# Layer 0 of an attention network: v's projection rebuilt as three one-pass products of split operands, and moved behind the third query/key block

## The chip, the cores and the metric

The kernel runs on one core of a Trainium2 chip. A core has a matrix engine (PE; its weight loads are listed apart as PEld), a vector engine (DVE), an activation engine (ACT), a general engine (POOL) and a sync engine (SP), which issues most of the DMA transfers. The metric is the device time of one execution in microseconds, as a median over runs; less is better.

## The reference, cut to what matters

The network has two layers over eight images of 384 channels and 32 x 32 pixels (1024 tokens). The change touches layer 0 alone: group norm, one projection to q, k and v, attention with a bias that depends on relative position, an output projection and a residual.

```
tokens = gn(x).reshape(b, c, n).transpose(0, 2, 1)           # 8 x 1024 x 384
qkv = (tokens @ qkv_w + qkv_b).reshape(b, n, 3, 8, 48)       # q, k, v: 384 columns each
attn = softmax(q * 48**-0.5 @ k.T + relative_bias)           # per head, 1024 x 1024
x = x + (attn @ v).reshape(b, n, c) @ proj_w + proj_b
```

Layer 1 (another attention and a feed-forward part, both with layer norms) follows and is not changed.

## The kernel before, in words

**Layer 0, image by image.** For each image the loop at the end of `_layer0` runs 32 attention units: four pairs of heads, two halves of the queries, four key groups (`m2`, 256 keys). A unit is `scores` (line 692: PE products of k and q into two PSUM tiles; line 703: DVE adds the position bias from `grow` and writes the tiles `e`; line 707: ACT takes the exponential in place) and, two units later, `weigh` (line 723: PE multiplies `e` with v into a PSUM tile). `weigh` of unit i-2 stands between the score products of unit i and the exponentials of unit i, so it is queued on PE right behind them. Every fourth `weigh` ends a half: ACT copies one part of the sum to `oT` (line 731), DVE adds the other (line 734), and after two halves `divide` starts a chain of small transfers, a power on POOL (line 752), and two units later a product on POOL (line 768).

**The projections of the next image** are made between the last unit of one image and the first unit of the next; this stretch is called a transition here. There are seven. q and k of images 1 to 7 are computed exactly in three cheap products: an fp32 number is cut into a high part (mask the last 12 bits, line 108, DVE), a low part (subtract, line 630, DVE) and a mixed part (line 112, DVE)[...]. ACT copies the high part into an fp32r tile (line 625). q and k have 768 columns, that is six blocks of 128; `_Cut.products` (line 170) makes for a block and one part 6 matmuls (3 chunks of channels, 2 halves of 512 tokens), so 18 a block, into two PSUM tiles `pg` (high and low) and `pm` (mixed). ACT (line 646) and DVE (line 650) join them into the q and k tile. The weights were cut in the same way during image 0 (`_cut_weights`) and lie in DRAM; three of the six blocks fit into SBUF (tag "w"), and `cuts.load` fetches the others in turn.

**v** is different: `project_v` (line 666) multiplies the normalised image with the fp32 weights `wv` directly, 24 matmuls of 128 x 128 by 384 an image; each is two instructions in the trace (48 records). DVE adds the bias (line 671). Its four groups stand at three places of the transition: group 0 between the last score products and the two `weigh` calls still held, group 1 after these, groups 2 and 3 between the third and the fourth q/k block.

**What sets the order.** Each engine runs its instructions in the order written. `later` is a list of jobs, each due after a number of steps; `later.step()` is called once a unit, once a q/k block and once a v group. PSUM holds four tiles of 128 x 1024 (`shared.ps`), which scores, sums and projections share. The pool of `e` tiles has nine buffers; in a transition all nine parts of the image lie in it. The image itself lies in a tile with the tag "x", one buffer, in the shared pool.

Of the kernel before, what the change touches and what calls it, by code (L numbers as in the profile page):

```python
# [19 lines left out]
F32 = mybir.dt.float32  # L20
F32R = mybir.dt.float32r
AF = mybir.ActivationFunctionType
ALU = mybir.AluOpType
# [4 lines left out]
P = 128  # L28
QP = P // 2
B, C, IH, IW = 8, 384, 32, 32  # L30
N = IH * IW
KC = C // P
MT = N // P
HALF = 512
# [3 lines left out]
H0, D0 = 8, 48  # L38
S0 = 64
# [24 lines left out]
CUT = 4096.0  # L64
# [41 lines left out]
def _masked(nc, out, of):  # L106

    nc.vector.tensor_single_scalar(out.bitcast(INT), of.bitcast(INT), MASK, op=ALU.bitwise_and)


def _mixed(nc, out, low, high):
    nc.vector.scalar_tensor_tensor(out, low, -CUT, high, ALU.mult, ALU.add)
# [63 lines left out]
class _Shared:  # L176
# [13 lines left out]
    def mm2(self, name):  # L190
        return self.ps.tile([P, NH, HALF], F32, tag="p", name=name)
# [8 lines left out]
class _Weights:  # L200
# [74 lines left out]
def _layer0(tc, ins, x1, sums, shared, weights, beside):  # L275
# [9 lines left out]
    with ExitStack() as ctx:  # L285
# [8 lines left out]
        def etile(name, shape=(P, N), dtype=F32):  # L294
            return ep.tile(list(shape), dtype, tag="e", name=name)
# [298 lines left out]

        BB = len(BLOCKS) // 2
        cut = dram.tile([len(BLOCKS), P, 3, KC, P], F32, tag="cut", name="cut", bufs=1)

        def cut_tile(name):
            return etile(name)[:, 0 : 2 * C]

        class Ahead:

# [3 lines left out]
            def __init__(self, b, xn):  # L606
                self.b, self.xn = b, xn
                self.qk = {}

            def tile(self, pair):  # L610
                if pair not in self.qk:
# [6 lines left out]
            def mask(self, k):  # L618
                _masked(nc, self.high(k), self.xn[:, k])

            def highs(self):
                self.parts = [[], [], []]
                for k in range(KC):
                    t = etile(f"xh{self.b}_{k}", dtype=F32R)
                    nc.scalar.copy(t, self.high(k))
                    self.parts[0].append(t)

            def low(self, k):
                t = etile(f"xl{self.b}_{k}", dtype=F32R)
# [5 lines left out]
                _mixed(nc, t, self.parts[1][k].bitcast(F32), self.high(k))  # L635
                self.parts[2].append(t)

            def project(self, cuts, n, order):
                pair, s = BLOCKS[n]
                t = self.tile(pair)[:, s]  # L640
                name = f"{self.b}_{pair}_{s}"
                ps = mm2("pg" + name), mm2("pm" + name)
                for i in order:
                    cuts.products(n, i, ps[i // 2], self.parts[i])
# [14 lines left out]
                later.step()  # L659

        def project_v(b, xn, some=range(MT // 2)):
            for m2 in some:
                pv = mm2(f"pv{b}_{m2}")
                for i in range(2):
                    for k in range(KC):
                        nc.tensor.matmul(  # L666
                            pv[:, i, 0:C], xn[:, k, ts(2 * m2 + i, P)], wv[:, k, :],
                            start=(k == 0), stop=(k == KC - 1),
                        )
# [190 lines left out]
        for k in range(KC):  # L860
            stages = _cut_weights(
                nc, k, plain[:, ts(k, 2 * C)],
                lambda name, k=k: (
                    spare if name == "ch" else plain[:, ts(k, 2 * C)] if name == "cl"
                    else cut_tile(f"{name}0{k}")
                ),
                cut,
            )
            for at, stage in zip(((9, 11, 13, 15), (20, 21, 22, 23), (24, 25, 26, 27))[k], stages):
                later.after(at + 1, stage)  # L870
        for b in range(B):
            held = []
            for i, u in enumerate(units):
                done = held.pop(0) if len(held) == LAG else None
                held.append(
                    (u, scores(b, qk, u, lambda: weigh(b, *done) if done else None))
                )
                if i == (12 if b == 0 else 1) and b + 1 < B:
                    xn = load(b + 1)
                    for at, stage in zip(  # L880
                        (5, 6, 7, 10, 13, *((14, 15) if b == 0 else (13, 13))),
                        group_norm(b + 1, xn),
                    ):
                        later.after(at, stage)
                if i == 3 and b > 0:
                    project_out(b - 1, residuals(b - 1, etile), range(NF0))
                if b == B - 1:
                    for at, work in beside:
                        if at == i:
                            work()  # L890
                later.step()
                if i == 28 and b == 0:
                    cuts = _Cut(
                        nc, cut, BLOCKS,
                        shared.pool.tile([P, KC * 3 * C], F32R, tag="w", name="wc"),
                    )
                    for n in range(BB):
                        cuts.load(n)
                if b in (1, 2, 3) and i == 12:
                    t = cut_tile(f"cw{b}")  # L900
                    weights.load_part(b - 1, t)
                    for at, stage in enumerate(
                        weights.cut(
                            b - 1, t, lambda name, b=b, t=t: t if name == "cl" else cut_tile(f"{name}1{b}")
                        )
                    ):
                        later.after(4 + at, stage)
                if b + 1 < B and i in (28, 29, 31):
                    if i == 28:
                        ahead = Ahead(b + 1, xn)  # L910
                    ahead.mask((28, 29, 31).index(i))
# [12 lines left out]
            def project(some):  # L924
                for n in some:
                    ahead.project(cuts, n, (0, 1, 2) if n == order[0] else (2, 0, 1))
                    if n in order[:BB]:
                        cuts.load((n + BB) % len(BLOCKS))

            ahead.highs()  # L930
            for k in range(2):
                ahead.low(k)
            project_v(b + 1, xn, [0])
            weigh_held()
            ahead.low(2)
            weigh_held()
            ahead.mixed(0)
            project_v(b + 1, xn, [1])
            for k in range(1, KC):
                ahead.mixed(k)  # L940
            project(order[:BB])
            project_v(b + 1, xn, [2, 3])
            project(order[BB:])
            qk = ahead.qk

        for m in range(KC):
# [1350 lines left out]
```

## Time and profile before

| what | value |
| --- | --- |
| median of 3 runs | 2976.45 us (2976.02 to 2978.29) |
| the profiled execution | 2973.66 us, span 2971.8 us |
| mean granted PE clock | 0.998 |
| PE busy | 2940.6 us (99%), 19370 instructions |
| DVE, ACT, POOL busy | 1940.2 us (65%), 1507.2 us (51%), 489.8 us (16%) |
| v's projection in layer 0 (line 666) | 384 records, 8 images |
| cut products of both layers (line 170) | 1396 records |

The span is what the profile covers; the 1.9 us between it and the execution's own time lie around it. A busy PE is not PE at its peak, since its ends are modelled and matmuls overlap; the spacing of starts tells more. In a timeline a row is a run of like instructions: start, length from the first start to the last end, engine, line, operation, output and inputs, shapes, count, and in brackets the idle time before the row with what ended it.

### The profile page before, as it was taken

The numbers are of one execution on the slowest core, as the hardware profiler recorded it, in microseconds if no ns is written. First come the engines' busy times: TensorE is split into PE (matmuls) and PEld (weight loads), VectorE is DVE, ScalarE is ACT, GpSimd is POOL, SyncE is SP. The second block draws the span as 40 slices with busy tenths as digits, with TensorE's granted clock in tenths as the row PEclk, the third lists the DMA queues.
The fourth block names the chain that finished last, engine by engine and source line by source line (L and its number), as shares of the span: only waits on it lengthen the run. The fifth ranks groups of instructions, "written<-read, shape, count | busy, mean of one in ns | idle before, by whom it ended". The sixth has DMA issues, their size and how long they took to land.

```text
span 2971.8 us, 47061 instructions
## 1 busy us (share of the span) xinstructions
PE 2940.6 (99%) x19370; PEld 1662.5 (56%) x19370; DVE 1940.2 (65%) x1937; ACT 1507.2 (51%) x1846; POOL 489.8 (16%) x312
## 2 busy tenths in 40 slices
PE   8999999999999999999999999999999999999998
PEld 3345555656565655644545656746747747655553
DVE  3775748575675747564565785775775775875756
ACT  2654626354453626354463564564564555564644
POOL 3020202111110202112202202301302302302020
PEclk9999999999999999999999999999999999999999
DMA  7532131312203130222411112202202112112111
GB/s 196 171 99 85 44 111 38 97 59 52 76 16 112 24 104 24 63 89 60 128 50 38 61 38 67 85 17 79 73 25 77 68 31 71 67 40 82 40 45 38
DMA packets 129520, 203.71 MB, mean 69 GB/s; under 512 B 61872, under 2 KB 79648, under 8 KB 128816
## 3 DMA queue, kind: packets, MB, share of 16 engines
q1 hardware_dynamic: 126032, 198.77, 22.9%
q8 instruction: 156, 2.56, 0.4%
q10 hardware_dynamic: 3264, 1.82, 0.2%
q14 instruction: 68, 0.56, 0.1%
HBM read 152.99 MB, written 38.51 MB: 64 GB/s over the span
## 4 chain that ended last, share of the span: by engine, by line
PE 91%; DVE 3%; DMA 2%; ACT 2%; issue 1%; SPq 0%; POOL 0%; DVEq 0%; ACTq 0%
PE s L692 15%; PE o L723 14%; PE s L1649 11%; PE o L1698 10%; PE pg L170 6%; PE y2p L1943 6%; PE y1p L1892 5%; PE pp L791 4%; PE pv L666 4%; PE pv L1586 4%; PE pm L170 3%; PE pp L1795 3%; PE pq L1438 1%; PE pq L572 1%; DMA rb<-rd 1%
## 5 line engine op out<-in xcount | busy, mean ns | idle before, releaser
L707 ACT ACTIVATE e<-e 128x1024 f32<-128x1024 f32 x512 | 535.3, 1057 | 357.0 <-DVE e L703 339.9
L703 DVE TENSOR_TENSOR e<-s,grow 128x1024 f32<-128x1024 f32 x512 | 601.2, 1218 | 164.4 <-PE s L692 156.5
L692 PE MATMUL s<-qk 48*64 48x512 f32 x4096 | 615.0, 592 | 7.6 <-DVE e L703 7.5
L723 PE MATMUL o<-e,v 64*64 64x512 f32 x4096 | 609.1, 590 | 0.0
L1660 ACT ACTIVATE e<-s,kc 128x512 f32<-128x512 f32 x768 | 463.9, 694 | 173.0 <-PE s L1649 163.4
L1649 PE MATMUL s<-qk,qk 64*64 64x512 f32 x3072 | 418.9, 592 | 1.8 <-DVE oT L1708 1.6
L1698 PE MATMUL o<-e,v 64*64 64x512 f32 x3072 | 414.5, 590 | 0.0
L692 PEld LDWEIGHTS s<-qk 48*64 48x64 f32 x4096 | 228.9, 132 | 250.9 <-issue 104.3
L723 PEld LDWEIGHTS o<-e,v 64*64 64x64 f32 x4096 | 244.8, 133 | 196.9 <-issue 113.8
L1649 PEld LDWEIGHTS s<-qk,qk 64*64 64x64 f32 x3072 | 154.0, 132 | 191.9 <-issue 109.2
L1675 DVE TENSOR_TENSOR t<-t,e 128x1024 f32<-128x1024 f32 x192 | 230.9, 1221 | 45.8 <-ACT e L1660 45.8
L1698 PEld LDWEIGHTS o<-e,v 64*64 64x64 f32 x3072 | 159.9, 133 | 168.9 <-issue 141.8
L752 POOL TENSOR_TENSOR inv<-sums,over 128x16 f32<-128x16 f32 x32 | 95.6, 2988 | 866.3 <-DMA sums<-sd 591.4
L1879 DVE TENSOR_REDUCE parts<-y 128x1 f32<-128x1024 f32 x75 | 89.7, 1217 | 103.4 <-ACT y L1876 103.0
L1672 DVE TENSOR_TENSOR t<-e,e 128x1024 f32<-128x1024 f32 x96 | 114.1, 1224 | 59.5 <-ACT e L1660 59.5
L1555 POOL TENSOR_TENSOR hc<-hc,rsqrt 128x32 f32<-128x32 f32 x24 | 138.2, 5757 | 2.0
L666 PE MATMUL pv<-wv,xn 128*128 128x384 f32 x384 | 128.9, 490 | 0.0
L1586 PE MATMUL pv<-wv,bx 128*128 128x384 f32 x384 | 128.3, 491 | 0.0
L1795 PE MATMUL pp<-oT,L_attn_proj_wT 128*128 128x512 f32 x288 | 126.3, 595 | 1.5 <-DVE oT L1761 1.5
L791 PE MATMUL pp<-oT,wp 128*128 128x512 f32 x288 | 125.7, 595 | 0.0
L650 DVE SCALAR_TENSOR_TENSOR qk<-pg,qk 128x1024 f32<-128x1024 f32 x42 | 51.5, 1225 | 112.8 <-PE pg L170 98.1
L1586 PEld LDWEIGHTS pv<-wv,bx 128*128 128x128 f32 x384 | 119.4, 314 | 9.8 <-ACT e L1660 4.1
(213 smaller groups left out, 3507.7 us busy)
## 6 DMA issues: line engine op xcount, KB each, us to landing
rb<-rd SPq DMA_DIRECT2D x110, 256.0 KB
wc<-there SPq DMA_DIRECT2D x25, 576.0 KB
wc<-cut SPq DMA_DIRECT2D x24, 576.0 KB
xn<-in_x_dram SPq DMA_DIRECT2D x24, 512.0 KB
res<-in_x_dram SPq DMA_DIRECT2D x24, 512.0 KB
x<-res SPq DMA_DIRECT2D x24, 512.0 KB
bx<-x SPq DMA_DIRECT2D x8, 1536.0 KB
rq<-hi SPq DMA_DIRECT2D x48, 256.0 KB
```

The lines of the kernel that those rows point to most:

```text
L170: self.nc.tensor.matmul(out[:, h], w[:, i, k], part[k][:, ts(h, HALF)], start=(k == 0 and i != 1), stop=(k == KC - 1 and i != 0),)
L666: nc.tensor.matmul(pv[:, i, 0:C], xn[:, k, ts(2 * m2 + i, P)], wv[:, k, :], start=(k == 0), stop=(k == KC - 1),)
L692: nc.tensor.matmul(s[j][ts(c, QP), i], qk[pair][rows, 1, ts(4 * m2 + 2 * i + c, QP)], qk[pair][rows, 0, ts(h, HALF)], start=True, stop=True,)
L703: nc.vector.tensor_add(e.rearrange("p (i q) -> p i q", i=2), s[j], bass.AP(near.tensor, near.offset, [near.ap[0], [-QROWS * IW, 2], [1, HA ...
L707: nc.scalar.activation(e, e, AF.Exp)
L723: nc.tensor.matmul(po[ts(j, S0), r], v[keys, 2 * m2 + i, 2 * pair + j, :], es[j][keys, ts(i, HALF)], start=(m2 == 0 and i == 0), stop=(m2 ...
L791: nc.tensor.matmul(pps[b, m][:, h], (wp[:, k] if k < NF0 else wl)[:, ts(m, P)], oT[:, k, ts(h, HALF)], start=(k == 0), stop=(k == (NF0 if ...
L1586: nc.tensor.matmul(pv[:, i, 0:C], xt[:, k].rearrange("c (p m) -> c m p", m=MT)[:, 2 * m2 + i], wv[:, k], start=(k == 0), stop=(k == KC - 1),)
L1649: nc.tensor.matmul(s[j][ts(c, QP), i], qk[pair, 1][rows, ts(4 * m2 + 2 * i + c, QP)], qk[pair, 0][rows, ts(h, HALF)], start=True, stop=True,)
L1660: nc.scalar.activation(e[:, ts(i, HALF)], s[j][:, i], AF.Exp, scale=kc[:, pair, j, m : m + 1])
L1675: nc.vector.tensor_add(total[j], total[j], e)
L1698: nc.tensor.matmul(po[ts(j, D1), r], v[keys, 2 * m2 + i, at : at + D1], es[j][keys, ts(i, HALF)], start=(m2 == 0 and i == 0), stop=(m2 == ...
```

## The change

For images 1 to 7, v is now projected from the same three parts as q and k. In image 0, `cut_weights_v` splits `wv` chunk by chunk (DVE: mask, subtract, and two steps later mix and scale) and SP stores the parts in DRAM (`cut_v`). At the first transition the high part is loaded into the place of `wv` (tag "wv") and stays; the low and mixed parts are loaded at every transition into the tile with tag "x", that is over the image, once its low parts are made. `project_v` of `Ahead` makes 18 one-pass matmuls of 128 x 128 by 384 for each of four groups, into two PSUM tiles, and DVE joins them with two operations for each 128 tokens instead of one.

The order of a transition changes too. The two held `weigh` calls now follow the score products at once. Then come the high and low products of the first two blocks, their mixed products, the third block, all four groups of v, and the other three blocks. From image 1 on the masks move from units 28, 29 and 31 to 25, 26 and 27, and the fp32r copies of the high parts on ACT from the transition to units 28, 29 and 30; at the first transition they stay where they were.

```diff
+        def cut_weights_v(k):
+            w = wv[:, k]
+            t = etile(f"cv{k}")
+            high, mixed = t[:, 0:C], t[:, HALF : HALF + C]
+            def first():
+                _masked(nc, high, w)
+                nc.sync.dma_start(cut_v[:, 0, k], high)
+                nc.vector.tensor_sub(w, w, high)
+            def second():
+                _mixed(nc, mixed, w, high)
+                nc.sync.dma_start(cut_v[:, 2, k], mixed)
+                nc.vector.tensor_scalar_mul(w, w, CUT)
+                nc.sync.dma_start(cut_v[:, 1, k], w)
+            first()
+            later.after(2, second)
...
+            def load_weights_v(self, wh):
+                t = shared.pool.tile([P, KC, N], F32R, tag="x", name=f"wx{self.b}")
+                t = t.rearrange("p k n -> p (k n)")[:, 0 : 2 * KC * C]
+                nc.sync.dma_start(
+                    t.bitcast(F32), cut_v[:, 1:3].rearrange("p i k c -> p (i k c)")
+                )
...
+            def project_v(self, m2):
+                ps = [mm2(f"v{g}{self.b}_{m2}") for g in "gm"]
+                for i in range(2):
+                    for part in (2, 0, 1):
+                        for k in range(KC):
+                            nc.tensor.matmul(
+                                ps[part // 2][:, i, 0:C],
+                                self.parts[part][k][:, ts(2 * m2 + i, P)], self.wv[part][:, k],
+                                start=(k == 0 and part != 1), stop=(k == KC - 1 and part != 0),
+                            )
+                for i in range(2):
...
+                    nc.vector.scalar_tensor_tensor(
+                        to, pm, -1.0 / CUT, bv.rearrange("p (h d) -> p h d", d=D0),
+                        ALU.mult, ALU.add,
+                    )
+                    nc.vector.scalar_tensor_tensor(
+                        to, pg, 1.0 + 1.0 / CUT, to, ALU.mult, ALU.add
+                    )
+                later.step()
...
+        for k in range(KC):
+            later.after(17 + k, lambda k=k: cut_weights_v(k))
...
-                if b + 1 < B and i in (28, 29, 31):
+                masks, rounds = ((28, 29, 31), ()) if b == 0 else ((25, 26, 27), (28, 29, 30))
...
-            ahead.highs()
+            if b == 0:
+                wh = const.tile([P, KC, C], F32R, tag="wv", name="wvh")
+                nc.sync.dma_start(wh.bitcast(F32), cut_v[:, 0])
+                for k in range(KC):
+                    ahead.round(k)
             for k in range(2):
                 ahead.low(k)
-            project_v(b + 1, xn, [0])
             weigh_held()
             ahead.low(2)
+            ahead.load_weights_v(wh)
             weigh_held()
-            ahead.mixed(0)
-            project_v(b + 1, xn, [1])
-            for k in range(1, KC):
+            for k in range(KC):
                 ahead.mixed(k)
-            project(order[:BB])
-            project_v(b + 1, xn, [2, 3])
-            project(order[BB:])
...
+            for n in order[:2]:
+                for i in range(2):
+                    ahead.products(cuts, n, i)
+            for n in order[:2]:
+                ahead.products(cuts, n, 2)
+                ahead.take(n)
+                load_behind(n)
+            for at, n in enumerate(order[2:], 2):
+                for i in (2, 0, 1):
+                    ahead.products(cuts, n, i)
+                ahead.take(n)
+                load_behind(n)
+                if at == BB - 1:
+                    for m2 in range(MT // 2):
+                        ahead.project_v(m2)
```

More of the change, by code (lines that the diff above doesn't have):

```diff
@@ L596, in _layer0 @@
         cut = dram.tile([len(BLOCKS), P, 3, KC, P], F32, tag="cut", name="cut", bufs=1)
+        cut_v = dram.tile([P, 3, KC, C], F32, tag="cutv", name="cutv", bufs=1)
         def cut_tile(name):
             return etile(name)[:, 0 : 2 * C]
+        def cut_weights_v(k):
[13 more added lines that the diff above has]
+            later.after(2, second)
         class Ahead:
@@ L608, in __init__ @@
                 self.qk = {}
+                self.parts, self.ps = [[], [], []], {}
             def tile(self, pair):
@@ L619, in mask, with round @@
                 _masked(nc, self.high(k), self.xn[:, k])
[L621 to L626, printed above, removed]
+            def round(self, k):
+                t = etile(f"xh{self.b}_{k}", dtype=F32R)
+                nc.scalar.copy(t, self.high(k))
+                self.parts[0].append(t)
             def low(self, k):
@@ L636, in mixed, with products, take @@
                 self.parts[2].append(t)
-            def project(self, cuts, n, order):
+            def products(self, cuts, n, i):
+                if (n, i // 2) not in self.ps:
+                    pair, s = BLOCKS[n]
+                    self.ps[n, i // 2] = mm2(f"p{'gm'[i // 2]}{self.b}_{pair}_{s}")
+                cuts.products(n, i, self.ps[n, i // 2], self.parts[i])
+            def take(self, n):
                 pair, s = BLOCKS[n]
                 t = self.tile(pair)[:, s]
[L641 to L644, printed above, removed]
+                ps = self.ps.pop((n, 0)), self.ps.pop((n, 1))
                 by = D0**-0.5 if s == 0 else 1.0
@@ L659, in project, with project_v @@
                 later.step()
-        def project_v(b, xn, some=range(MT // 2)):
-            for m2 in some:
+            def load_weights_v(self, wh):
[4 more added lines that the diff above has]
+                )
+                t = t.rearrange("p (i k c) -> p i k c", i=2, k=KC)
+                self.wv = wh, t[:, 0], t[:, 1]
+            def project_v(self, m2):
[9 more added lines that the diff above has]
+                for i in range(2):
+                    to = v[:, 2 * m2 + i, :, SP:S0]
+                    pg, pm = (p[:, i, 0:C].rearrange("p (h d) -> p h d", d=D0) for p in ps)
+                    nc.vector.scalar_tensor_tensor(
[6 more added lines that the diff above has]
+                later.step()
+        def project_v(b, xn):
+            for m2 in range(MT // 2):
                 pv = mm2(f"pv{b}_{m2}")
@@ L907, in _layer0 @@
                         later.after(4 + at, stage)
-                if b + 1 < B and i in (28, 29, 31):
-                    if i == 28:
+                masks, rounds = ((28, 29, 31), ()) if b == 0 else ((25, 26, 27), (28, 29, 30))
+                if b + 1 < B:
+                    if i == masks[0]:
                         ahead = Ahead(b + 1, xn)
-                    ahead.mask((28, 29, 31).index(i))
+                    if i in masks:
+                        ahead.mask(masks.index(i))
+                    if i in rounds:
+                        ahead.round(rounds.index(i))
             def weigh_held():
@@ L922, in _layer0, with load_behind @@
             order = [n % len(BLOCKS) for n in range(b % 2 * BB, b % 2 * BB + len(BLOCKS))]
[L924 to L928, printed above, removed]
-            ahead.highs()
+            if b == 0:
[3 more added lines that the diff above has]
+                    ahead.round(k)
             for k in range(2):
                 ahead.low(k)
-            project_v(b + 1, xn, [0])
             weigh_held()
             ahead.low(2)
+            ahead.load_weights_v(wh)
             weigh_held()
-            ahead.mixed(0)
-            project_v(b + 1, xn, [1])
-            for k in range(1, KC):
+            for k in range(KC):
                 ahead.mixed(k)
-            project(order[:BB])
-            project_v(b + 1, xn, [2, 3])
-            project(order[BB:])
+            def load_behind(n):
+                if n in order[:BB]:
+                    cuts.load((n + BB) % len(BLOCKS))
+            for n in order[:2]:
[11 more added lines that the diff above has]
+                if at == BB - 1:
+                    for m2 in range(MT // 2):
+                        ahead.project_v(m2)
             qk = ahead.qk
```

## The prediction

> **What bounds the kernel now.** First the page's busy times:
>
> ```profile
> span 2971.8 us, 47061 instructions
> PE 2940.6 (99%) x19370; PEld 1662.5 (56%) x19370; DVE 1940.2 (65%) x1937; ACT 1507.2 (51%) x1846; POOL 489.8 (16%) x312
> ...
> PE 91%; DVE 3%; DMA 2%; ACT 2%; issue 1%; SPq 0%; POOL 0%; DVEq 0%; ACTq 0%
> ```
>
> PE is never idle for long, and the chain that ended last is 91% PE (last line). So PE work taken out of a transition comes off the end, if nothing then keeps PE waiting. Next the timeline of PE in the first transition (image 0 to 1), with ACT's rows in a second block:
>
> ```profile
> 188.81 0.59 PE L692 MATMUL s<-qk 48*64 48x512 f32 x1
> ...
> 190.97 2.16 PE L723 MATMUL o<-e,v 64*64 64x512 f32 x15
> 193.06 4.14 PE L666 MATMUL pv<-wv,xn 128*128 128x384 f32 x12
> 197.12 3.66 PE L723 MATMUL o<-e,v 64*64 64x512 f32 x32
> 200.72 4.14 PE L666 MATMUL pv<-wv,xn 128*128 128x384 f32 x12
> 204.40 1.84 PE L170 MATMUL pg<-xh,wc 128*128 128x512 f32 x6
> 206.08 1.56 PE L170 MATMUL pg<-xl,wc 128*128 128x512 f32 x6
> ...
> 217.28 7.90 PE L666 MATMUL pv<-wv,xn 128*128 128x384 f32 x24
> ...
> 237.70 5.92 PE L692 MATMUL s<-qk 48*64 48x512 f32 x45
> ```
>
> ```profile
> 192.77 2.20 ACT L707 ACTIVATE e<-e 128x1024 f32<-128x1024 f32 x2 [1.13 <-DVE e L703]
> 194.86 2.92 ACT L625 CAST xh<-qk 128x1024 fp32r<-128x1024 f32 x3
> ```
>
> Spacing: one record of v's fp32 matmul lasts 0.486 modelled, so 24 records are (7.90 - 0.486)/23 = 0.322 us apart. A one-pass product of 512 columns: (1.56 - 0.396)/5 = 0.233 us. From the first score product of unit 31 (188.81) to that of the next image (237.70) it is 48.89 us: scores and a `weigh` up to 192.97 (4.16), v 48 x 0.3225 = 15.48, two `weigh` 3.44, six blocks 108 x 0.2335 = 25.22, and some 0.6 at switches. The same interval in the other six transitions: 50.05, 48.84, 50.02, 49.91, 49.67, 49.55. What makes five of them longer is in the timeline of unit 30 of image 1:
>
> ```profile
> 355.51 2.37 POOL L768 TENSOR_TENSOR oT<-oT,rb 128x1024 f32<-128x1024 f32 x1 [6.37 <-DVE e L703]
> 356.53 1.91 DVE L108 TENSOR_SCALAR qk<-xn 128x1024 int32<-128x1024 int32 x1
> 359.62 1.51 PE L692 MATMUL s<-qk 48*64 48x512 f32 x11 [0.79 <-DVE e L703]
> ```
>
> The mask takes 0.68 elsewhere; here it ends 0.56 after POOL's product, so it stood behind it. The bias add behind the mask is late, and PE has no free PSUM tile. The same mask takes 1.88, 1.79, 1.56 and 1.43 in images 3 to 6. Last, DVE in image 0, units 17 to 20, where work is added:
>
> ```profile
> 141.79 2.36 DVE L703 TENSOR_TENSOR e<-s,grow 128x1024 f32<-128x1024 f32 x2 [0.39 <-PE s L692]
> 144.08 0.69 DVE L734 TENSOR_TENSOR oT<-o,oT 128x512 f32<-128x512 f32 x1
> 144.68 1.28 DVE L513 BATCH_NORM_STATS2 gst<-xn 128x6 f32<-128x512 f32 x2
> 145.88 2.34 DVE L703 TENSOR_TENSOR e<-s,grow 128x1024 f32<-128x1024 f32 x2
> 148.13 1.27 DVE L513 BATCH_NORM_STATS2 gst<-xn 128x6 f32<-128x512 f32 x2
> 149.33 2.34 DVE L703 TENSOR_TENSOR e<-s,grow 128x1024 f32<-128x1024 f32 x2
> 152.57 1.23 DVE L703 TENSOR_TENSOR e<-s,grow 128x1024 f32<-128x1024 f32 x1 [0.90 <-PE s L692]
> ```
>
> Here DVE runs without a gap from 141.79 to 151.67; it, not PE, sets the pace.
>
> [...] In the trace the first two loads of a v group are 0.108 us apart[...]
>
> **The change part by part.**
>
> *v's products.* Out: 15.48 us a transition. In: 4 groups x 18 = 72 one-pass matmuls of 384 columns, a form the trace doesn't have. [...] Upper end: the 233.5 of 512 columns, if it isn't the columns that set it. I take 178: 12.82 us, so 2.66 less, times 7: **-18.6**. Ends: [...]233.5 gives +9.3.
>
> *The masks.* At units 25 to 27 no POOL product runs in the transitions shown (it comes in unit 30); POOL's power in unit 27 (3 us) didn't hold a DVE scaling of 0.55 that ran inside it in image 0 (179.97). The five long transitions lose their excess over 48.87: 1.18 + 1.15 + 1.04 + 0.80 + 0.68 = **-4.8**. Ends: -4.8 and 0 (mask 25 falls behind an `oT` sum and another POOL operation holds it).
>
> *The copies of the high parts.* Three a transition go to units 28 to 30 on ACT, 0.95 us apart in a row. A unit lasts 3.44 us and ACT needs 2 x 1.06, at most 0.59 for `oT`, and now 1.0: 3.7 once, 3.2 otherwise. The exponentials of unit 31 begin when DVE has added (ACT idles 1.1 us before them now), so they aren't later. Zero; end +1 a transition (7) if they are.
>
> *No v group ahead of the held `weigh` calls.* Behind the last copy of the exponentials now stands `weigh` of unit 31: PE ends unit 29's at 192.97 and unit 30's at 194.69, but ACT ends the last exponential at 192.77 + 2.20 = 194.97. PE waits some 0.35. DVE's low parts (from 194.32, 1.15 apart, third after unit 30's `weigh`) are done about 198; PE needs them 1.4 us after `weigh` 31's end at 196.8. Mixed parts follow DVE's `oT` sum, from about 198.5 to 202; PE has 4 x 1.4 = 5.6 us of high and low products of two blocks before them, up to 202.4. In transition 1, where the copies still follow the exponentials, the third ends at 197.8, needed at 197.8. The third block takes over the PSUM tile of the first one's mixed product; from the start of those 6 products ACT begins 1.74 later (207.48 to 209.22) and takes 1.12, against 2.80 for both mixed products: 0.15. Switches between types drop from 0.6 to 0.3. Net 0.2 x 7: **+1.4**; ends 0 and +7.
>
> *The weights of v.* 1.18 MB issued on SP when the third low part is made, about 9 us into the transition, behind no other wait; needed after two `weigh`, three blocks: 4.16 + 3.44 + 54 x 0.2335 + 0.5 = 20.7. Three loads of 590 KB moved from 183.9 to about 192 with some other traffic, 250 to 300 GB/s, so 4 to 5 us and 2 of latency: there at 16. If it were late, it would cost its lateness seven times. SP's `sd` and q/k stores queue behind it, and these wait for DVE results that come later anyway. The block loads are issued earlier than before, and have v's 12.8 us to land in. The first transition adds 590 KB ahead of it, under the same cover.
>
> *Joining v.* 4 DVE operations a group, near 0.55 each (128x384 addition: 0.553), 2.2 us under 3.2 us of PE; before, 1.1 of 3.9. Hidden.
>
> *Cutting wv in image 0.* Per chunk on DVE: mask and scale (0.55 at 768 columns, 0.68 at 1024, so 0.35 at 384), subtract and mix (0.95 and 1.22, so 0.545): 1.8 us, 1.45 at back-to-back spacing. They come after the bias additions of units 16 (first of chunk 0), 17, 18 (also the second of chunk 0), 19 and 20. Unit 16's, 0.8, has a gap of 0.39 ahead; those of 17 and 18, 0.8 and 1.6, none; unit 19's falls into the gap of 0.90, unit 20's mostly into one of 0.6. Exposed: 0.4 + 0.8 + 1.6 + 0.2 = **+3.0**; ends +1.5 and +5.5 (all of it). The nine stores (1.77 MB, units 17 to 21) hold three `e` buffers, about two units each; the next users come three units later.
>
> Sum: -18.6 - 4.8 + 1.4 + 3.0 = -19.0. On the profiled execution 2973.66 (span 2971.8 and 1.9 around it) that gives 2954.7. The median lies 2.8 above that execution, and I carry the offset: 2976.45 - 19.0 = **2957.4**.
>
> **Rivals.** *A product of 384 columns costs what one of 512 does.* 72 x 0.2335 = 16.8 us, 1.3 more than v now: +9.3 instead of -18.6, total +8.9, 2985. [...] Against: a load is only 0.108 us[...]. It decides from a spacing of (15.48 + 0.06)/72 = 0.216 us on, where the whole gain is gone. *v's weights late*: at 100 GB/s, as the mixed traffic about 225 moved, 12 us and 2 of latency put them at 23, 2.3 late x 7 = 16: 2973. Against: the large contiguous loads ran at 250. *ACT and DVE can't hold the end of the attention*: no gain from masks (4.8) and 1 us lost a transition (7): 2969. *The cheaper product isn't reached by the path*, since DVE and ACT become the bound in the transition: they were busy 18.7 and 10.1 of the 45 us from 195 to 240, and DVE gets 8 operations of 0.55 more. Discarded.
>
> **How the numbers follow.** Main case 0.79: 2951 to 2964 by its bounds. Rival 1 0.07, rival 2 0.05, rival 3 0.06, the rest 0.03, both ways. Range 2949 to 2969. This measurement can't tell less than 0.2%, 6 us, from nothing. Faster: the main case, rival 3 and a part of rival 2, 0.87; same 0.05; slower 0.08.
>
> **What would show it.** The new v rows: 36 matmuls of 384 columns, spacing 0.176 to 0.180 us. Transitions near 46.4 us, alike to 0.3. No mask over 0.7 in units 25 to 27 and no PE wait for DVE in unit 30. A wait of 0.2 to 0.5 before the last `weigh`. In image 0 three longer units, 17 to 19. Wrong if the spacing is over 0.2, if PE waits for a DMA before v's first product, or if score products wait for DVE in units 26 to 30.

## The result, and the profile after

The changed kernel takes 2957.8 us (median of 6 runs, 2955.07 to 2959.49) against 2977.37 for the kernel before beside it (6 runs, 2974.22 to 2979.95): 0.9934 of its time, with a 95% interval of 0.9923 to 0.9946. The forecast was 2957.4. Beside each other the two medians differ by 19.6 us, where 19.0 was forecast. Repeated on another chip, further down, the ratio was 0.9934 again (0.9920 to 0.9947).

The total agrees to 0.4 us, but the transitions and image 0 are each off by about 3 us, with opposite signs. The spans of the two profiled executions differ by 18.8 us, and three stretches account for it:

| stretch | before | after | difference | forecast |
| --- | --- | --- | --- | --- |
| seven transitions, first score product of unit 31 to that of the next image | 346.9 us | 321.8 us | -25.1 us | -22.0 us |
| image 0, first score product of unit 0 to that of unit 31 | 113.4 | 119.3 | +5.9 | +3.0 |
| start of image 0 | 75.4 | 75.9 | +0.5 | 0 |

The page of the changed kernel, the same lines as were shown of before:

```profile
span 2953.0 us, 47525 instructions
...
PE 2920.5 (99%) x19538; PEld 1694.0 (57%) x19538; DVE 1970.4 (67%) x2005; ACT 1505.0 (51%) x1846; POOL 491.5 (17%) x312
...
PE 91%; DVE 3%; DMA 2%; ACT 2%; issue 1%; SPq 0%; POOL 0%; DVEq 0%; ACTq 0%
```

The chain is still 91% PE and PE is still busy 99% of the time: 20 us of its work are gone, and no other engine has taken over. The timeline of PE in the first transition (start, length, engine and line, operation, shapes, count):

```profile
197.31 5.98 PE L777 MATMUL o<-e,v 64*64 64x512 f32 x47
...
216.17 0.69 PE L698 MATMUL vm<-wx,xd 128*128 128x384 f32 x3
...
228.66 1.55 PE L170 MATMUL pm<-xd,wc 128*128 128x512 f32 x6
```

All 72 products of v, one record each where an fp32 product of v had two, stand in one block, from 216.17 to 228.66: 12.49 us, so 0.1735 us each (0.1733 in the next transition), against 15.48 us for v before. No row of this stretch, up to the next image's first score product at 241.34, has an idle time in brackets. The row from 197.31 holds the last three `weigh` calls, the two held ones among them. Its products start in groups of four, 0.43 us from group to group. One distance differs: the first group of the last `weigh` starts 0.77 us after the group before it (200.58 to 201.35). That is the wait for the last exponential, 0.34 us, and it is 0.34 in each of the seven transitions; the row shows no gap for it because the records before it, with their modelled ends, reach over it. ACT's row of that exponential, which ends at 201.30:

```profile
199.11 2.19 ACT L761 ACTIVATE e<-e 128x1024 f32<-128x1024 f32 x2 [1.13 <-DVE e L757]
```

The timeline of DVE at the end of image 1's attention, with the masks in their new units (the last one is shown):

```profile
352.54 0.68 DVE L108 TENSOR_SCALAR qk<-xn 128x1024 int32<-128x1024 int32 x1
...
360.58 2.35 DVE L757 TENSOR_TENSOR e<-s,grow 128x1024 f32<-128x1024 f32 x2 [0.33 <-PE s L746]
```

This is the mask of unit 27; those of units 25 and 26 take 0.68 and 0.69 us, where one had taken 1.91. POOL's product of unit 30 (359.32 to 361.70) meets none of them, and DVE then waits for PE, not PE for DVE. Last, DVE in image 0, within units 19 to 22:

```profile
152.04 0.54 DVE L112 SCALAR_TENSOR_TENSOR cv<-wv,cv 128x384 f32<-128x384 f32 x1
152.62 0.36 DVE L616 TENSOR_SCALAR wv<-wv 128x384 f32<-128x384 f32 x1
...
155.16 0.55 DVE L112 SCALAR_TENSOR_TENSOR cv<-wv,cv 128x384 f32<-128x384 f32 x1
...
163.57 1.23 DVE L757 TENSOR_TENSOR e<-s,grow 128x1024 f32<-128x1024 f32 x1 [2.18 <-PE s L746]
```

The first two lines, chunk 0, are what the forecast described: mixing (line 112) and scaling (616) stand between other work on a DVE that had no gap, and the bias additions come later. The third is the mixing of chunk 1. The pieces take 0.35 to 0.56 us, as estimated. The last line isn't in the forecast: one bias addition comes after DVE has stood idle for 2.18 us. The trace names the score product as what it waited for, but that had ended at 159.80, so another semaphore was the last. The addition writes an `e` buffer. The queue of SyncE shows who held it (line 818 loads for the division, line 615 stores parts of v's weights):

```profile
157.48 1.09 SPq L818 DMA_DIRECT2D rb<-rd  x2
158.66 0.53 SPq L615 DMA_DIRECT2D cutv<-cv  x1
```

The second store of chunk 1 (line 615) reads that buffer. Its data, the third line above, were ready on DVE at 155.71, but it was issued at 158.66, behind the division's store (155.73) and loads (157.48). PE's unit 22 lasts 6.18 us instead of 3.57. The lengths of image 0's units 16 to 23, from the starts of their score products:

| kernel | 16 | 17 | 18 | 19 | 20 | 21 | 22 | 23 |
| --- | --- | --- | --- | --- | --- | --- | --- | --- |
| before | 10.38 | 3.61 | 3.66 | 3.75 | 3.45 | 3.44 | 3.57 | 4.16 |
| after | 10.56 | 3.67 | 3.97 | 4.60 | 5.18 | 3.69 | 6.18 | 4.06 |

Units 17 to 21 are 3.2 us longer, most of it in units 18 to 20, and unit 22 is 2.6 us longer.

### The profile page after: what moved, and what is told of

It reads as the page before. It is cut to its first block, busy times and chain, and to the rows that moved or that the text cites. A ratio compares the mean times of both kernels' runs of the same rounds, so it can differ in the third digit from the quotient of the medians.

```text
span 2953.0 us, 47525 instructions
## 1 busy us (share of the span) xinstructions
PE 2920.5 (99%) x19538; PEld 1694.0 (57%) x19538; DVE 1970.4 (67%) x2005; ACT 1505.0 (51%) x1846; POOL 491.5 (17%) x312
## 4 chain that ended last, share of the span: by engine, by line
PE 91%; DVE 3%; DMA 2%; ACT 2%; issue 1%; SPq 0%; POOL 0%; DVEq 0%; ACTq 0%
PE s L746 15%; PE o L777 15%; PE s L1722 11%; PE o L1771 11%; PE pg L170 6%; PE y2p L2016 6%; PE y1p L1965 5%; PE pp L845 4%; PE pv L1659 4%; PE pm L170 3%; PE pp L1868 3%; PE vg L698 2%; PE pq L1511 2%; PE pq L572 1%; PE vm L698 1%; DVE qk L1592 1%
## 5 line engine op out<-in xcount | busy, mean ns | idle before, releaser
L1745 DVE TENSOR_TENSOR t<-e,e 128x1024 f32<-128x1024 f32 x96 | 114.1, 1224 | 57.7 <-ACT e L1733 57.7
L1965 PE MATMUL y1p<-lun,w 128*128 128x512 f32 x360 | 113.5, 396 | 2.4 <-DVE lun L1915 2.4
```

Of the source, the lines that this page charges most:

```text
L1965: nc.tensor.matmul(py[m][:, h], w1[:, k, ts(m, P)], un[k][i][:, ts(h, HALF)], start=(k == 0 and i == 0), stop=(k == KC - 1 and i == 1),)
```

## The experiments

Times are medians, ratios are to the kernel before on the same chip with the 95% interval. The transitions of each kernel that bears on them, in us:

| kernel | 0-1 | 1-2 | 2-3 | 3-4 | 4-5 | 5-6 | 6-7 | sum |
| --- | --- | --- | --- | --- | --- | --- | --- | --- |
| before | 48.89 | 50.05 | 48.84 | 50.02 | 49.91 | 49.67 | 49.55 | 346.9 |
| masks early alone | 48.88 | 48.82 | 48.82 | 48.82 | 48.80 | 48.81 | 48.81 | 341.8 |
| changed, v in fp32 | 49.15 | 48.91 | 48.97 | 48.91 | 48.93 | 48.89 | 48.93 | 342.7 |
| changed | 46.19 | 45.92 | 45.97 | 45.93 | 45.96 | 45.89 | 45.94 | 321.8 |
| changed, masks late | 45.72 | 46.96 | 47.19 | 46.99 | 47.54 | 47.18 | 46.84 | 328.4 |
| changed, not interleaved | 47.78 | 47.03 | 47.01 | 47.01 | 46.99 | 47.00 | 47.01 | 329.8 |
| changed, v's weights late | 52.75 | 51.57 | 52.62 | 51.71 | 52.87 | 51.84 | 53.07 | 366.4 |

**Masks early, alone**

```diff
-                if b + 1 < B and i in (28, 29, 31):
-                    if i == 28:
+                masks = (28, 29, 31) if b == 0 else (25, 26, 27)
+                if b + 1 < B and i in masks:
+                    if i == masks[0]:
```

> The kernel before with one edit: in images 1 to 6 the three masks of the next image's x stand behind units 25, 26, 27 instead of 28, 29, 31. Nothing else of the change is in it. The prediction's step 2: the stretches from unit 31 to the next image of 50.05, 50.02, 49.91, 49.67 and 49.55 us fall to 48.8 to 48.9, because no mask overlaps GpSimd's multiply any more (each mask 0.68 to 0.70 us), the two of 48.84 stay, units 25 to 27 stay at 3.44: 4.8 us less in all, 2972 to 2973. Rival A, the end of attention has no room (R3): units 25 to 27 grow by 0.2 to 0.7 each in six images, 4 to 10 us given back, 2974 to 2982. Rival B, the long stretches come from something else (transfers, the take): they stay between 49.5 and 50.1, 2977.

Measured: 2968.74 us, 0.9978 (0.9968 to 0.9988), 6.0 us below the kernel before beside it (2974.78). The transitions of images 1 to 6 are all 48.80 to 48.82, and units 25 to 27 stay at 3.44. That is 5.2 us less in the transitions, where 4.8 was forecast; both rivals fall. The span of this execution is 6.0 us shorter too; of the rest, 0.3 is in the start of image 0 and 0.6 behind layer 0's last image, where the edit changes nothing.

**Masks and copies late**

```diff
-                masks, rounds = ((28, 29, 31), ()) if b == 0 else ((25, 26, 27), (28, 29, 30))
+                masks, rounds = (28, 29, 31), ()
...
-                for k in range(KC):
-                    ahead.round(k)
+            for k in range(KC):
+                ahead.round(k)
```

> The changed kernel with its steps 2 and 3 undone: masks behind units 28, 29, 31 and the three fp32r copies on ScalarE behind unit 31, in all images; the cut of v's weights, its products and their order stay. By the prediction's step 2 the stretches of 45.9 to 46.2 us of images 1, 3, 4, 5, 6 grow by 0.7 to 1.2 each and that of image 2 by nothing: 4.8 us more than the changed kernel, near 2962.5; a mask near a GpSimd multiply takes 1.2 to 1.8 us instead of 0.68. Rival A, the copies' move was worth something too: the six stretches all grow, by 0.5 to 1 each beyond that, 2965 to 2969. Rival B, what the changed kernel gained was v's products alone, and the order of masks is hidden: within 1 us of the changed kernel, 2957 to 2959.

Measured: 2963.14 us, 0.9955 (0.9939 to 0.9970). Against the changed kernel the six transitions that the edit touches grew by 1.04, 1.22, 1.06, 1.58, 1.29 and 0.90, which is 7.1. (The first one, which it leaves as it was, came out 0.5 shorter; why is not shown.) Rival B falls. Rival A expected the copies to cost on top of the masks. The lengths of the masks show that they don't. This is the timeline around unit 30 of image 1 in this kernel:

```profile
362.78 2.38 POOL L822 TENSOR_TENSOR oT<-oT,rb 128x1024 f32<-128x1024 f32 x1 [6.37 <-DMA rb<-rd]
...
364.00 1.70 DVE L108 TENSOR_SCALAR qk<-xn 128x1024 int32<-128x1024 int32 x1
```

The mask takes 1.70 us, 1.01 over its 0.69. In the six images the masks of unit 29 exceed 0.69 by 1.01, 1.16, 1.04, 1.56, 1.26 and 0.85 us; each transition's growth is within 0.06 us of its mask's. So the masks explain all of it but 0.06 us a transition at most, and the move of the copies is worth no more than that; zero was forecast. What I had wrong in the expectation is image 2: here its mask collides too (1.85 us). In the kernel before, that mask started at 526.69 and POOL's product at 526.70; the mask took its 0.68, and it was the product that took longer, 2.91 us instead of 2.38. In this kernel the product starts first, at 529.99, and the mask at 531.08. In both kernels the one that started second took longer than it does elsewhere. This kernel's profiled execution is the longest of its four, 2969.16 us, and its image 0 took 122.2 us, which the note on the clock below comes back to.

**v in fp32 at its new place**

```diff
-                    for m2 in range(MT // 2):
-                        ahead.project_v(m2)
+                    project_v(b + 1, xn)
```

The cut of v's weights in image 0 and the loads of its parts are not in this kernel either, since nothing uses them.

> The changed kernel with v's projection as one fp32 product again (48 matmuls of 128x384), at its new place behind the third block; v's weights are not cut in image 0 and not loaded. Masks, copies and the interleaved first two blocks stay as in the changed kernel. The forecast's account: the v part of a transition takes 15.4 to 15.5 us instead of 12.48, so each of the seven stretches is 3.0 us longer, 48.9 to 49.0; image 0 goes back from 119.3 to 113.4 between unit 0 and unit 31. Against the changed kernel 21.0 - 5.9 = 15 us more, 2973, and 4 to 5 below before. Rival A, the order and not the parts brought the gain (interleaving, v behind the third block): 2958 to 2965. Rival B, the longer units of image 0 have nothing to do with the cut: image 0 stays near 119, 2978 to 2979.

Measured: 2970.01 us, 0.9981 (0.9973 to 0.9990), 4.8 us below the kernel before beside it. The transitions sum to 342.7, 20.9 above the changed kernel: 2.99 each. Image 0 takes 113.4 us again. From v's first product to the second row behind v's block it is 395.22 - 378.36 = 16.86 us here, and 396.08 - 382.22 = 13.86 in the changed kernel:

```profile
378.36 15.64 PE L720 MATMUL pv<-wv,xn 128*128 128x384 f32 x48
...
395.22 1.10 PE L170 MATMUL pg<-xh,wc 128*128 128x512 f32 x4
```

The gain is the product of v itself, and both rivals fall. Set beside the kernel with early masks alone, this one is 0.9 us worse in its transitions: the new order with the old product isn't a gain.

**The first two blocks not interleaved**

```diff
-            for n in order[:2]:
-                for i in range(2):
-                    ahead.products(cuts, n, i)
-            for n in order[:2]:
-                ahead.products(cuts, n, 2)
-                ahead.take(n)
-                load_behind(n)
-            for at, n in enumerate(order[2:], 2):
-                for i in (2, 0, 1):
+            for at, n in enumerate(order):
+                for i in (0, 1, 2) if at == 0 else (2, 0, 1):
```

> The changed kernel with the first two blocks' products not interleaved by parts: each block runs high, low, mixed (the later ones mixed, high, low) before the next begins. The mixed parts of x are ready at 10.5, 11.7 and 12.9 us after unit 31's first score and the first block asks for them at 10.8: TensorE waits 0.4 to 0.6 us twice, 1.0 to 1.2 us in each of seven transitions, and they take 47.0 to 47.2 us instead of 45.9; 7 to 8 us more than the changed kernel, 2965 to 2966. Rival, the wait is met by slack elsewhere (the take of the first block begins earlier and frees its sums earlier): within 1 us of the changed kernel, 2957 to 2959.

Measured: 2964.81 us, 0.9956 (0.9939 to 0.9973); transitions +8.0 in all. The timeline of PE in the second transition shows where:

```profile
374.36 0.73 PE L170 MATMUL pm<-xd,wc 128*128 128x512 f32 x2 [0.24 <-DVE xd L112]
375.50 2.13 PE L170 MATMUL pm<-xd,wc 128*128 128x512 f32 x8 [0.40 <-DVE xd L112]
```

PE asks for the second and the third chunk of the mixed parts before DVE has made them. The starts of consecutive products are 0.63 and 0.80 us apart there instead of 0.23: 0.97 us, of the 1.11 that the transition grew. In the kernel before, a group of v stood between the two held `weigh` calls and the first block, so PE had other work at this place. I read the interleaving as paying for the wait that moving v opens; no run tests it without that move.

**v's columns divided otherwise**

```diff
+                    for at, end in (((0, C),), ((0, 192), (192, C)), ((0, 256), (256, C)), ((0, 320), (320, C)))[m2]:
...
-                                ps[part // 2][:, i, 0:C],
+                                    ps[part // 2][:, i, at:end],
```

> The changed kernel with the columns of v's one-pass products divided otherwise in each of the four groups of a transition: first group 384 as it is; second 192 and 192; third 256 and 128; fourth 320 and 64. The distance of products tells what a column costs. If a product costs in proportion to its columns (233.5 ns at 512, 173.3 at 384, so 0.45 to 0.46 ns each): 320 take 144 to 147 ns, 256 take 115 to 117, and below some 108 ns, where the load of 128x128 weights takes longer than the product, 192, 128 and 64 columns all cost about 108. The groups then take 18 x 173 = 3.1 us, 36 x 108 = 3.9, 18 x (116 + 108) = 4.0 and 18 x (146 + 108) = 4.6. Rival A, a fixed part in each product (173.3 and 233.5 give 0.47 ns per column, so a fixed part of minus 7: this would need another form): 256 and 320 columns lie off the line by over 10 ns. Rival B, no floor from the weight load: 192 cost 87 ns, 128 cost 58, 64 cost 29, and all groups take 3.1 us.

This kernel was run for the distances alone (one execution, 2980.06 us). The timeline of PE in the second transition, rows of two sizes, each with the row behind it:

```profile
386.81 0.68 PE L699 MATMUL vm<-wx,xd 128*128 128x384 f32 x3
387.33 0.68 PE L699 MATMUL vg<-wvh,xh 128*128 128x384 f32 x3
...
397.40 0.60 PE L699 MATMUL vg<-wx,xl 128*128 128x320 f32 x3
397.84 0.42 PE L699 MATMUL vm<-wx,xd 128*128 128x64 f32 x3
```

A row is three products, so the distance of two starts by three is what one costs: 0.173 us for 384 columns, 0.147 for 320, and by rows read in the same way 0.117 for 256. From 384 columns down to 256, and with the 0.2335 of 512 last, that is 0.451, 0.458, 0.457 and 0.456 ns a column: in proportion, without a fixed part. Below that a floor holds. Products of 192 columns came 0.111 to 0.113 us apart, and those of 64 and 128 columns 0.111 to 0.112 where they follow their own kind. The four groups took 3.13, 4.00, 4.10 and 4.62 us, as the main account of the expectation had it, and both rivals fall. That the load of the weights sets the floor fits the 0.108 us between the first two loads of a v group in the kernel before, but no run tests it alone.

**v's weights loaded late**

```diff
             ahead.low(2)
-            ahead.load_weights_v(wh)
...
                 ahead.take(n)
+                if n == order[0]:
+                    ahead.load_weights_v(wh)
```

> The changed kernel with the load of v's low and mixed weights (1.18 MB) issued behind the first block's take instead of ahead of the last weigh. The stores of that take are issued some 18 us after unit 31's first score, so the load is issued at about 19 and lands 5.1 us later, at 24, while the products ask for it at 20.8. Account: TensorE waits 3 to 4.5 us ahead of v's products in each of seven transitions, which take 49 to 50.4 us instead of 45.9: 21 to 31 us more, 2979 to 2989. This is the prediction's rival R2 made to happen. Rival, the load is not what v's products wait for (the wait shown by the trace is for sums or VectorE): transitions within 1 us of 45.9, 2957 to 2965.

Measured: one execution, with a span of 3001.6 us against 2953.0, outside both expectations. The wait itself is as expected: in the trace's list of what waited for the tile `wx`, v's products stand 28.6 us in seven waits, 4.1 each. But the transitions grew by 44.6. The remaining 16.0 are in the rows behind the wait; the timeline of PE, and then one line of the table by stretches (length, busy time of PE, its weight loads, DVE, ACT and POOL, then the granted clock of PE, the DMA share and GB/s):

```profile
395.85 1.30 PE L698 MATMUL vm<-wx,xd 128*128 128x384 f32 x3 [4.05 <-DMA wx<-cutv]
396.94 1.16 PE L698 MATMUL vg<-wvh,xh 128*128 128x384 f32 x3
397.90 1.10 PE L698 MATMUL vg<-wx,xl 128*128 128x384 f32 x3
```

```profile
395.70:398.80 3.10, 2.95 (x9) 2.98 (x10) 0.00 (x0) 0.00 (x0) 0.00 (x0) 0.50 0.30 106
```

After 4.05 us without work PE's granted clock was 0.50, and the first nine products came 0.32 us apart instead of 0.173; in the third transition about sixteen did. In this kernel a wait of 4 us cost 5.7 to 7.1. The prediction's rival of late weights charged the lateness alone, 2.3 us a transition; for a wait of 4 us that would have been too little. The load's place about 12 us ahead of its use keeps it from happening.

**One held buffer taken out of image 0**

```diff
-            t = etile(f"cv{k}")
-            high, mixed = t[:, 0:C], t[:, HALF : HALF + C]
+            if k == 1:
+                high, mixed = plain[:, 0:C], plain[:, C : 2 * C]
+            else:
+                t = etile(f"cv{k}")
+                high, mixed = t[:, 0:C], t[:, HALF : HALF + C]
```

> The changed kernel with one edit: the parts of the second chunk of v's weights stand in the space of layer 0's query and key weights, which is free by then, instead of a buffer of the exponentials' ring; same instructions, same place in time. Account: unit 22 of image 0 (6.18 us against 3.57 before) waited for that buffer, whose last store sat in the queue of SyncE behind the division's store and loads. Then unit 22 falls to 3.5 to 4.2, unit 0 to 31 of image 0 takes 116.6 to 117.4 us instead of 119.3, and the time is 2955 to 2955.8. Rival A, the wait of unit 22 is VectorE's own backlog from units 18 to 20: unit 22 stays at 5.5 to 6.2, 2957.8. Rival B, it moves on: another held buffer (the first or third chunk's) stops unit 21, 22 or 23 by as much, 2957.8.

Measured: 2954.1 us, 0.9918 (0.9902 to 0.9935). DVE at the place where it had stopped:

```profile
160.04 2.35 DVE L760 TENSOR_TENSOR e<-s,grow 128x1024 f32<-128x1024 f32 x2
162.30 0.68 DVE L791 TENSOR_TENSOR oT<-o,oT 128x512 f32<-128x512 f32 x1
```

The two bias additions follow each other without a gap, and unit 22 takes 3.73 us: the buffer was what it waited for, and both rivals fall. Image 0 as a whole takes 117.7, not 116.6 to 117.4: units 16 to 18 were 1.2 us longer in this execution than in the changed kernel's, because a table transfer that unit 16 waits for landed later. DVE waited 6.29 us for it here and 5.11 in the changed kernel; the edit does not touch it.

**The cut moved into the stop of unit 16**

```diff
-        for k in range(KC):
-            later.after(17 + k, lambda k=k: cut_weights_v(k))
...
+        later.after(25, cut_weights_v)
...
+            for k in range(KC):
+                _masked(nc, high, w)
+                nc.vector.tensor_sub(w, w, high)
+                _mixed(nc, mixed, w, high)
+                nc.vector.tensor_scalar_mul(w, w, CUT)
...
+            later.after(1, store)
```

> The changed kernel with the cutting of v's weights moved: all twelve VectorE operations (5.2 us) stand in a row ahead of the table copy of image 0's unit 16, where VectorE waits 5.1 us for a transfer in any case, and the nine stores are issued one unit later, so that the three buffers are let go three units before their next users. Account of the trace: the 5.9 us that image 0 grew are VectorE time in full units plus a wait of 2.2 us for a buffer held by a queued store, nothing else. Then image 0 takes 113.3 to 114.0 us from unit 0 to 31 instead of 119.3, and the time is 2951.8 to 2953, 5 to 6 below the changed kernel. Rival A, the cost is the stores on the queue (nine issues of 0.38 us delay the loads and stores behind them wherever they stand): units 16 to 19 grow by 2 to 4 us in sum, 2955 to 2957. Rival B, the wait at unit 16 ends later with VectorE's extra work (the transfer was not what it waited for): 5 us more there, no gain, 2957 to 2958.

Measured: 2951.15 us, 0.9917 (0.9903 to 0.9930). DVE at the stop, with the last piece of the cut, and later, at unit 22:

```profile
132.78 0.36 DVE L611 TENSOR_SCALAR wv<-wv 128x384 f32<-128x384 f32 x1
133.06 0.64 DVE L498 COPY grow<-oT 128x480 f32<-128x480 f32 x1
...
156.88 2.35 DVE L756 TENSOR_TENSOR e<-s,grow 128x1024 f32<-128x1024 f32 x2 [0.61 <-PE s L745]
```

The twelve operations, from 126.86 on, fill the time in which DVE of the changed kernel stands 5.11 us for a transfer, and the copy comes 0.7 us later than in the changed kernel. Nearly all of that is the first mask, which takes 1.00 us instead of 0.35: POOL's product of 2.38 us had begun 1.59 before it. Units 19 to 22 are 3.73, 3.45, 3.44 and 3.57 again, and image 0 takes 114.1 us, 0.7 over the kernel before. Both rivals fall. It was run once more beside the changed kernel on one chip:

> The changed kernel as it is, timed beside the next one on the same chip. 0.9934 of the kernel before; seven transitions of 45.9 to 46.2 us, unit 22 of image 0 between 5.8 and 6.5 us, unit 0 to 31 of image 0 near 119.

> The changed kernel with the cutting of v's weights in the stop of image 0's unit 16, as run before. If the 5.1 us that its trace saved in image 0 hold, it is 4 to 6 us below the changed kernel on the same chip, 0.9914 to 0.9920 of the kernel before, with unit 22 at 3.57 us and image 0 at 114. If the saving was one execution's, the two agree within 1.5 us.

Measured: changed 2956.85 us, 0.9934 (0.9920 to 0.9947); with the cut in the stop 2950.2 us, 0.9914 (0.9900 to 0.9927). The medians differ by 6.7 us and the two sets of five runs don't overlap (the highest is 2952.66, the lowest of the changed kernel 2954.23). Unit 22 took 6.09 us in the one and 3.57 in the other; image 0 took 119.5 and 115.4. The saving holds, but two figures of the expectation don't: image 0 was to take 114, and the medians were to differ by 4 to 6. In image 0, units 16 and 17 took 11.84 and 4.16 us, against 11.14 and 3.44 in the first run of this kernel, and PE's granted clock was 0.50 for 10.2 us around the stop instead of 6.8. The two profiled executions differ by 4.5 us of span, 4.1 of them in image 0; the profiled one with the cut in the stop was the slowest of its five, so what the medians differ by beyond that is in no trace. This version beats both kernels.

## Why the prediction was right, and where it was not

**v's products** (forecast -18.6 from 178 ns, upper end 233.5): right in kind, mis-sized. A product of 384 columns takes 173.3 ns, and the seven transitions lost 20.9 us by it (the kernel with v in fp32), 2.3 more than forecast. The step that failed is the price of 178, which was an estimate of mine that no row of the trace shows. For this type the spacing measured here is 0.451 to 0.458 ns a column at 256, 320, 384 and 512 columns, without a fixed part. Scaling the measured row, 233.5 x 384/512 = 175.1, would have come nearest. Rival 1, the same price as 512 columns, is excluded by the 173.3 itself, and the sizes 256 and 320 lie on the same line.

**The masks** (-4.8): -5.2 alone, and 7.1 when undone in the changed kernel. That the masks do it is shown, since their lengths and those of the transitions move together to 0.06 us. Begun behind POOL's product the mask took 1.43 to 2.25 us, away from it 0.68 to 0.70; in image 2 of the kernel before the mask began first, and the product took 2.91 us instead of 2.38. No trace shows why the later one takes longer.

**The copies** (0): shown to be 0, within 0.06 us a transition.

**The transition's new order** (+1.4): the kernel with v in fp32 stands 0.9 us above the one with early masks alone, over seven transitions. PE's wait ahead of the last `weigh` was 0.34 us each time, within the 0.2 to 0.5 forecast. Seven of them are 2.4 us, so the new order also saves some 1.4 elsewhere. The forecast looked for a saving in fewer switches between types; no run measures that part alone. That the interleaving keeps this term small is shown by the 8.0 us that it costs to leave it out.

**v's weights** (0): right. The load was issued at 369.80 us in the second transition and its traffic ended near 374.9; it was needed at 382.22. No wait. The forecast's 16 us into the transition was about 2.5 later than the traffic's end, on the safe side. For the 2 us of latency in it the kernel before has a measured 1.78: a load of 8 KB issued at 203.76, and the work on POOL that waits for it starting at 205.54.

**Joining v** (hidden): right. No two products of v start more than 0.18 us apart in any of the seven transitions.

**Cutting wv** (+3.0, ends 1.5 and 5.5): measured +5.9, outside the ends. The sum of the pieces was right, 3.2 in units 17 to 21, though units 18 to 20 grew and not 17 to 19. The sentence that failed is "The nine stores (1.77 MB, units 17 to 21) hold three `e` buffers, about two units each; the next users come three units later". The buffer was held until its store had read it, not only until DVE had made the part at 155.71. The second store of chunk 1, issued at 158.66, stood behind the division's store and loads in the queue of SyncE, which the prediction named for the transition alone. Taking that one buffer away brought unit 22 from 6.18 to 3.73 us.

The products (-20.9), the masks (-5.2) and the order (+0.9) make up the -25.1 of the transitions; they do so by construction, since each is the step between two neighbours in a row of four kernels: before, masks early alone, changed with v in fp32, changed. With +5.9 in image 0 and +0.5 ahead of it this is -18.7 of the -18.8. So the mechanisms of the forecast were right but for the held buffer. That the total came within 0.4 us is luck: it needed two misses of 3 us that cancelled.

## What to carry to other kernels

Price a new size of a matmul by scaling the nearest measured row of the same type; here that gives 175.1 ns where 173.3 was measured, and the price stopped falling at 0.11 us, below 256 columns. When a store borrows a buffer from a ring, its hold ends when the store has been issued and has read it (here the part was ready at 155.71, and its store was issued at 158.66): read the queue that issues it, for the units concerned, and count from there. And look for a stop of an engine on a transfer that is there anyway. In this kernel, work placed in it made image 0 longer than before by 0.7 and 2.0 us in two executions, and the same work a few units later by 5.9 and 6.1.

## What the runs showed of the hardware that I had not expected

Some pauses of PE cost more than their length. In the kernel with v's weights late the granted clock was 0.50 after each of the 4.1 us waits, for 3.41 us in three transitions, which grew by 5.7 to 6.0 us, and for 6.83 in the other four, which grew by 6.6 to 7.1. The clock also fell after a shorter pause, at the stop of unit 22 in image 0. In the kernel with late masks PE stood 2.29 us there, and the table of stretches shows what followed; beside it the changed kernel, where it stood 1.55 us (the granted clock is the third number from the end):

```profile
168.50:171.70 3.20, 3.17 (x16) 1.13 (x20) 3.20 (x5) 0.98 (x1) 0.87 (x3) 0.54 0.01 5
```

```profile
164.90:167.00 2.10, 2.06 (x17) 0.87 (x18) 2.10 (x4) 0.99 (x1) 0.00 (x0) 1.00 0.02 8
```

With v's weights late PE stood 2.04 us at the same stop, and the granted clock was 0.50 from 169 to 172 us. The stop of unit 16 in image 0 brought it to 0.50 for 6.83 us in the kernel before, where PE stood 4.17 us, and for 6.83 us in the changed one, where it stood 4.35. How short a pause may be, and what counts beside its length, these readings don't show.
